# Where the first attention stage ends: its memory freed in three steps, and the layers' first projections moved between its last products

## The chip, the cores and the metric

The kernel runs on one core of a Trainium2 chip. The metric is the device time of one execution in microseconds (us); lower is better. The engines are named as in the profile: PE (matrix products; PEld is its loading of weights), DVE (vector), ACT (scalar), POOL (GpSimd) and SP, which here only issues DMAs.

## What is computed

The input x has 4 batches of 512 tokens with 128 features. It goes through a causal attention block, and then through six layers, each of a local attention (windows of 32 tokens, looking back one window) and a gated feed-forward part. The result of the six layers is added to what went into them.

```python
...
    x = x + _L0_attn_ref(_layernorm(x, axis=-1), L0_attn_Wq, L0_attn_Wk, L0_attn_Wv, L0_attn_Wr)
    x = x + _L0_ffn_ref(_layernorm(x, axis=-1), L0_ffn_Wqkv, ...)
...
        for i in range(DEPTH):
            x = attn_layer(shift_tokens(x), Wqkv[i], q_scale[i], k_scale[i], Wo[i]) + x
            x = ffn_layer(shift_tokens(x), ln_g[i], ln_b[i], W1[i], b1[i], W2[i], b2[i]) + x
```

In the first block `q`, `k` and `v` have 16 heads of 64; the softmax rows times `v` are projected out by `Wr`. In a layer `q` and `k` are divided by their norm, scaled and rotated by position before the scores. `shift_tokens` moves half of the features by one token. All is in float32, apart from masks.

## The kernel before

The program is one sequence per engine, written out by hand: inside `tc.manual_schedule()` each engine executes its instructions in the order in which the code issues them, and a tile library puts in the waits that the tiles' reads and writes ask for. When a memory pool is given back and a new one takes its place, the first users of the new tiles wait for the last users of the old ones that lie there.

Stage one (L132 to L364) works on batches b = 0 to 3 and on eight pairs of heads c = 0 to 7. A step m of its loop handles two blocks of 128 rows: scores on PE (L216), the mask as a further product (L229), row maximum on DVE (L241), exponents on ACT (L247), scaling on POOL (`normalise`, L259), and, one step later, transposes of the exponents (L270) with their copies out of PSUM by ACT (L274) and DVE (L276). Two steps later `times_v1` multiplies with V in two halves (L287) and DVE copies the result (L297). When a batch is through, `project_out1` multiplies by `Wr` (L302, 8 products that accumulate), and DVE adds the block's input (L303) to give `x1T[b]`. The layers' input is the normalised `x1T[b]`; `norm_x1` does that in three steps: mean (L93 on PE, L95 on DVE, L97 on ACT), variance (L102 on PE, then 15 small operations on DVE: L104 and `rsqrt`, L79 to L85) and scale (L110 on PE, L114 on DVE). For batches 0 to 2 the steps are spread over the next batch's loop; for batch 3 they come after the stage ("late").

[...] Stage one uses one for projections (`ps_pj`), two for transposes (`ps_pt`), four for scores (`ps_sc`), one for the product with V (`ps_o`). The layers use four for projections (`ps_proj`, two buffers of two), two for attention (`ps_att`) and two single ones (`ps_one`).

After the loop stand the rest of the products with V (L366 to L368) and the last `project_out1`. Then all of stage one's memory is given back, the layers' pools are made (L372), and POOL clears the borders of three tiles (L493, L496, L499).

The layers' work is cut into units: a unit is a layer i, a batch b and a block T of 128 tokens, 96 in all. `begin` makes the shifted input `xs` on POOL (L413 to L415) and, for batch 0, the rotation tables `lt` of the layer (a DMA of scales, L420, and one product on POOL, L422). `slot(n)` issues work of four units at once: the scores and products of unit n, the output of n-1, the transposes of q and k of n+1, the projections of n+2. Its order is the order of the code at L727 to L787. A projection (`project`, L439) is followed by Square on ACT (L450), the sum of squares (L455) and the two halves of the rotation (L460, L464) on DVE, their addition on POOL (L475), the inverse norms (DVE L479, L79, L80, then 12 small operations on POOL, L82 to L85) and the scaling by them on POOL (L483). `v_windows` copies V out on ACT (L517) and sends it by 16 DMAs on SP into overlapping windows (L525 to L529). Scores are L562 (mask) and L573, their maximum L583, the difference L585, exponents L591; the products with V are L605.

The loop starts at n = -2, so that slot -2 holds the projections of unit 0 alone, slot -1 those of unit 1 and the transposes of unit 0, and slot 0 the first scores:

```python
        for n in range(-2, len(units) + NT + 3):
            if -2 <= n < 1:
                late[n + 2]()
```

Of the kernel before, what the change touches and what calls it, by code (L numbers as in the profile page):

```python
# [8 lines left out]
F32 = mybir.dt.float32  # L9
# [3 lines left out]
ALU = mybir.AluOpType  # L13
AX = mybir.AxisListType

P = 128
HEADS = 16
HD = 64
# [13 lines left out]
def body(ctx: ExitStack, tc: tile.TileContext, a, out: bass.AP):  # L32
# [98 lines left out]

    with tc.tile_pool(name="s1", bufs=1) as s1, tc.tile_pool(  # L132
        name="ps1", bufs=1, space=bass.MemoryType.PSUM
    ) as ps1, tc.manual_schedule():
        wq = s1.tile([P, INNER], F32, tag="wq", name="wq")
        wk = s1.tile([P, INNER], F32, tag="wk", name="wk")
        wv = s1.tile([P, INNER], F32, tag="wv", name="wv")
        wr = s1.tile([P, NC, EMB], F32, tag="wr", name="wr")
        pen = s1.tile([P, S], BF16, tag="pen", name="pen")
# [13 lines left out]
        def bank1():  # L153
            return ps1.tile([P, 512], F32, tag="pj", name="ps_pj", bufs=1)

# [5 lines left out]
        def load_x(b):  # L161
            xp = pt_bank()
            for t in range(NT):
                nc.tensor.transpose(xp[:, t * P : (t + 1) * P], xr[b][:, t, :], ident)
            x0T[b] = s1.tile([P, S], F32, tag=f"x0T{b}", name=f"x0T{b}")
            nc.scalar.copy(x0T[b], xp)
# [23 lines left out]
        def make_v(b, j, t):  # L190

            if t == 0:
                vs[b, j] = s1.tile([P, NT, 512], F32, tag="v1", name="v1", bufs=3)
            p = bank1()
            mm(
                p,
                lhsT=xnT[b][:, t * P : (t + 1) * P],
                rhs=wv[:, j * 512 : (j + 1) * 512],
                start=True,
                stop=True,  # L200
            )
            nc.vector.tensor_copy(vs[b, j][:, t, :], p)

        class Rows:
# [58 lines left out]
            def transposes(self):  # L263
                b, c, t = self.b, self.c, self.t
                if t == 0:
                    pTs[b, c] = s1.tile([P, 2, NT, S], F32, tag="pT1", name="pT1", bufs=2)
                for h in range(2):
# [10 lines left out]
        def times_v1(b, c, half):  # L278

            if half == 0:  # L280
                os_[b, c] = ps1.tile([P, S], F32, tag="o1", name="ps_o1", bufs=1)
            o = os_[b, c]
# [12 lines left out]
            if half == 1:  # L295
                at = aTs[b, c] = s1.tile([P, S], F32, tag="aT1", name="aT1", bufs=NC + 2)
                nc.vector.tensor_copy(at, o)  # L297

        def project_out1(b):
            y = bank1()  # L300
            for c in range(NC):
                mm(y, lhsT=wr[:, c, :], rhs=aTs.pop((b, c)), start=(c == 0), stop=(c == NC - 1))  # L302
            nc.vector.tensor_tensor(x1T[b], y, x0T[b], ALU.add)  # L303

# [15 lines left out]
        for m in range(last + 1):  # L320
# [41 lines left out]
            if b > 0 and c == 1 and odd:  # L362
                project_out1(b - 1)
                norms1[b - 1] = norm_x1(bank1, b - 1)  # L364
            if b in range(1, B) and not odd and 4 <= c <= 6:
                norms1[b - 1][c - 4]()  # L366

        times_v1(B - 1, NC - 2, 1)  # L368
        for half in range(2):
            times_v1(B - 1, NC - 1, half)  # L370
        project_out1(B - 1)


    s2 = ctx.enter_context(tc.tile_pool(name="s2", bufs=1))
    ps = ctx.enter_context(tc.tile_pool(name="ps2", bufs=1, space=bass.MemoryType.PSUM))

# [25 lines left out]
    def one_t():  # L402
        return ps.tile([P, 512], F32, tag="one", name="ps_one", bufs=2)

# [3 lines left out]
    def flat(pt):  # L408
        return pt.rearrange("p a n -> p (a n)")

    def shift_into(dst, src):

        nc.gpsimd.memset(dst[HD:P, 0:1], 0.0)  # L413
        nc.gpsimd.tensor_copy(dst[0:HD, :], src[0:HD, :])
        nc.gpsimd.tensor_copy(dst[HD:P, 1:S], src[HD:P, 0 : S - 1])  # L415

    def layer_tables(i):

        scales = s2.tile([P, 4 * HD], F32, tag="scales", name="scales")
        nc.sync.dma_start(out=scales, in_=a["scales"][i : i + 1].to_broadcast([P, 4 * HD]))  # L420
        lt = s2.tile([P, NT, 4, HD], F32, tag="lt", name="lt", bufs=2)
        nc.gpsimd.tensor_tensor(  # L422
            lt.rearrange("p t f d -> p t (f d)"),
            tabs.rearrange("p t f d -> p t (f d)"),
            scales.unsqueeze(1).to_broadcast([P, NT, 4 * HD]),
            ALU.mult,
        )
        return lt

# [18 lines left out]
    def square(u, j):  # L448
        u.sq = s2.tile([P, INNER], F32, tag="t1", name="sq", bufs=3)
        nc.scalar.activation(u.sq, u.p[j], AF.Square)  # L450
# [6 lines left out]
    def rotate(u, j):  # L457
        t0 = u.r[j] = s2.tile([P, INNER], F32, tag="rot", name="rot", bufs=6)
        lt, pf, half = u.lt, u.p[j], HD // 2
        nc.vector.tensor_tensor(  # L460
            heads(t0), heads(pf), lt[:, u.T, 2 * j].unsqueeze(1).to_broadcast([P, HEADS, HD]), ALU.mult
        )
        t1 = u.t1 = s2.tile([P, INNER], F32, tag="t1", name="t1", bufs=3)
        nc.vector.tensor_tensor(  # L464
# [9 lines left out]
    def add_rotated(u, j):  # L474
        nc.gpsimd.tensor_tensor(u.r[j], u.r[j], u.t1, ALU.add)  # L475
# [6 lines left out]
    def over_norm(u, j):  # L482
# [5 lines left out]
        )  # L488

    kT_first = s2.tile([P, NC, W + P], F32, tag="kT_first", name="kT_first")
    nc.gpsimd.memset(kT_first[:, :, 0:W], 0.0)  # L493
    vw_first = s2.tile([P, NW, NC, HD + 1], F32, tag="vw_first", name="vw_first")
    for c in range(2):
        nc.gpsimd.memset(vw_first[c * HD : c * HD + W, 0], 0.0)  # L496
    vts = [s2.tile([P, 2, NC, HD + 1], F32, tag=f"vt{j}", name=f"vt{j}") for j in range(2)]
    for t_ in vts:
        nc.gpsimd.memset(t_[:, :, :, HD : HD + 1], 1.0)  # L499

# [5 lines left out]
    def new_vw(u):  # L506
        if u.T == 0:
            return vw_first
        return s2.tile([P, NW, NC, HD + 1], F32, tag="vw", name="vw", bufs=3)

# [29 lines left out]
    def transpose_q(u):  # L540
        u.qT = s2.tile([P, NC, P], F32, tag="qT", name="qT", bufs=1)
        for g in range(2):
            transposed(u.r[0], g, u.qT, 0)
# [168 lines left out]
    def begin(u):  # L712

        if u is None or u.T:
            return
        xs = s2.tile([P, S], F32, tag="xs", name="xs", bufs=2)
        shift_into(xs, xT[u.b])
        lt = layer_tables(u.i) if u.b == 0 else units[u.n - 1].lt
        for v in units[u.n : u.n + NT]:
            v.xs, v.lt, v.p = xs, lt, [None] * 3  # L720

    def do_project(u, j):
        u.p[j] = project(u, j)
        if u.b + 1 == B and u.T + 1 == NT and u.i + 1 < L:
            wpart[j] = load_part(u.i + 1, j)

    def slot(n, now, last):  # L727
# [8 lines left out]
        if new:  # L736
            do_project(new, 0)
            square(new, 0)
        if u:
            exponents(u)  # L740
# [35 lines left out]
        if new:  # L776
            rotate(new, 1)
            add_rotated(new, 1)
            over_norm(new, 1)
        if nxt:  # L780
            carry_k(nxt, follower(nxt))
# [7 lines left out]
    with tc.manual_schedule():  # L789
        begin(units[0])  # L790
        ffns = {}
        late = norm_x1(one_t, B - 1)
        for n in range(-2, len(units) + NT + 3):
            if -2 <= n < 1:
                late[n + 2]()
            q = n // NT - 1
# [96 lines left out]
```

## Time and profile before

| what | us |
|---|---|
| median of 3 runs | 2374.94 |
| lowest, highest run | 2371.28, 2376.27 |
| the profiled execution, its own time | 2373.12 |
| its span, first to last instruction | 2371.3 |
| end of stage one's last output product | 590.9 |
| start of the first scores of slot 0, 1, 2, 3 | 621.4, 640.6, 656.6, 673.4 |

The profile is one execution. In a timeline or chain the first number is the start in us from the span's start and the second the duration; `x8` counts instructions. PE's records count a float32 product twice. A stretch's PEclk is the share of full clock that was granted to TensorE. The slots that follow repeat in a pattern of four, some 17 to 19.5 us each, up to 2327 us.

### The profile page before, as it was taken

The numbers are of one execution on the slowest core, as the hardware profiler recorded it, in microseconds if no ns is written. First come the engines' busy times: TensorE is split into PE (matmuls) and PEld (weight loads), VectorE is DVE, ScalarE is ACT, GpSimd is POOL, SyncE is SP. The second block draws the span as 40 slices with busy tenths as digits, with TensorE's granted clock in tenths as the row PEclk, the third lists the DMA queues.
The fourth block names the chain that finished last, engine by engine and source line by source line (L and its number), as shares of the span: only waits on it lengthen the run. The fifth ranks groups of instructions, "written<-read, shape, count | busy, mean of one in ns | idle before, by whom it ended". The sixth has DMA issues, their size and how long they took to land.

```text
span 2371.3 us, 81682 instructions
## 1 busy us (share of the span) xinstructions
PE 2222.6 (94%) x35056; PEld 1448.1 (61%) x35088; DVE 1696.8 (72%) x2692; ACT 1301.6 (55%) x2166; POOL 1436.9 (61%) x1897
## 2 busy tenths in 40 slices
PE   6999999998789999999999999999999999999997
PEld 3555555554466666666666666666666666666664
DVE  3665656655778777777777778777878777777774
ACT  2554444543345566655665656566556666565662
POOL 2453434443776677666767766767766767766760
PEclk9999999999899999999999999999999999999999
DMA  3000000000222232222332223223232223322220
GB/s 110 1 1 1 1 1 1 1 1 1 62 67 57 62 91 64 64 72 59 82 73 62 65 64 87 67 62 73 68 85 63 68 59 85 77 55 69 66 59 15
DMA packets 91026, 125.82 MB, mean 53 GB/s; under 512 B 25262, under 2 KB 39468, under 8 KB 90668
## 3 DMA queue, kind: packets, MB, share of 16 engines
q1 hardware_dynamic: 90236, 119.02, 20.5%
q8 instruction: 280, 4.59, 0.9%
q10 hardware_dynamic: 432, 1.57, 0.2%
q14 instruction: 78, 0.64, 0.1%
HBM read 20.41 MB, written 1.05 MB: 9 GB/s over the span
## 4 chain that ended last, share of the span: by engine, by line
PE 77%; DVE 14%; issue 3%; ACT 3%; POOL 1%; DMA 1%; SPq 0%; ACTq 0%; POOLq 0%
PE ps_proj L439 19%; PE ps_one L535 10%; PE ps_one L630 7%; PE ps_att L605 6%; PE ps_att L573 6%; PE ps_sc L216 5%; PE ps_o L287 4%; PE ps_pt L270 3%; PE ps_proj L663 3%; PE ps_proj L664 3%; PE ps_proj L677 2%; DVE on L615 2%; DVE yt L79 2%; ACT vt L517 1%; DVE rot L460 1%
## 5 line engine op out<-in xcount | busy, mean ns | idle before, releaser
L439 PE MATMUL ps_proj<-wqkv,xs 128*128 128x512 f32 x1152 | 570.1, 618 | 31.5 <-ACT vt L517 22.9
L475 POOL TENSOR_TENSOR rot<-rot,t 128x1024 f32<-128x1024 f32 x192 | 453.3, 2361 | 199.3 <-DVE t L464 197.2
L259 POOL TENSOR_TENSOR pr<-pr,den 128x1024 f32<-128x1024 f32 x128 | 241.1, 1894 | 333.9 <-DVE den L256 331.7
L450 ACT ACTIVATE sq<-ps_proj 128x1024 f32<-128x1024 f32 x192 | 196.9, 1025 | 407.5 <-PE ps_proj L439 354.3
L483 POOL TENSOR_TENSOR rot<-rot,ss 128x1024 f32<-128x1024 f32 x192 | 365.4, 1903 | 15.1
L439 PEld LDWEIGHTS ps_proj<-wqkv,xs 128*128 128x128 f32 x1152 | 199.6, 191 | 220.1 <-issue 156.3
L455 DVE TENSOR_REDUCE ss<-sq 128x16 f32<-128x1024 f32 x192 | 233.1, 1214 | 53.8 <-ACT sq L450 53.5
L241 DVE TENSOR_REDUCE nm<-ps_sc 128x2 f32<-128x1024 f32 x128 | 156.1, 1219 | 118.8 <-PE ps_sc L229 118.8
L460 DVE TENSOR_TENSOR rot<-ps_proj,lt 128x1024 f32<-128x1024 f32 x192 | 233.6, 1217 | 0.0
L464 DVE TENSOR_TENSOR t<-ps_proj,lt 128x1024 f32<-128x1024 f32 x192 | 233.1, 1214 | 0.0
L274 ACT COPY pT<-ps_pt 128x512 f32<-128x512 f32 x128 | 75.2, 588 | 263.2 <-PE ps_pt L270 261.4
L630 PEld LDWEIGHTS ps_one<-aT,wo 128*128 128x128 f32 x1536 | 186.3, 192 | 45.3 <-issue 44.5
L82 POOL TENSOR_TENSOR yt<-y 128x32 f32<-128x32 f32 x288 | 69.3, 241 | 237.7 <-DVE y L80 222.7
L535 PE MATMUL ps_one<-ident,rot 128*128 128x128 f32 x1536 | 211.3, 281 | 0.8 <-ACT qT L538 0.7
L583 DVE TENSOR_REDUCE mx<-ps_att 128x16 f32<-128x1024 f32 x96 | 117.6, 1225 | 119.8 <-PE ps_att L573 119.8
L630 PE MATMUL ps_one<-aT,wo 128*128 128x128 f32 x1536 | 187.3, 275 | 0.4 <-ACT aT L538 0.4
L247 ACT ACTIVATE pr<-ps_sc,nm 128x512 f32<-128x512 f32 x256 | 175.0, 695 | 16.5 <-DVE nm L241 16.5
L535 PEld LDWEIGHTS ps_one<-ident,rot 128*128 128x128 f32 x1536 | 165.7, 142 | 20.5 <-issue 2.9
L614 DVE RECIPROCAL rden<-ps_att 128x8 f32<-128x8 f32 x192 | 39.6, 206 | 193.5 <-PE ps_att L605 192.0
L605 PEld LDWEIGHTS ps_att<-vw,pT 64*32 64x32 f32 x9216 | 105.1, 105 | 106.4 <-issue 72.8
L605 PE MATMUL ps_att<-vw,pT 64*32 64x65 f32 x9216 | 129.0, 225 | 35.5 <-DVE on L615 28.9
L270 PEld LDWEIGHTS ps_pt<-ident,pr 128*128 128x128 f32 x1024 | 119.2, 141 | 55.3 <-issue 44.9
(127 smaller groups left out, 4042.1 us busy)
## 6 DMA issues: line engine op xcount, KB each, us to landing
vw<-vt SPq DMA_DIRECT2D x1152, 65.0 KB
vw_first<-vt SPq DMA_DIRECT2D x336, 65.0 KB
wqkv<-in_wqkv_dram SPq DMA_DIRECT2D x18, 512.0 KB
wo<-in_wo_dram SPq DMA_DIRECT2D x6, 512.0 KB
w<-in_w_dram SPq DMA_DIRECT2D x6, 341.0 KB
xr<-in_x_dram SPq DMA_DIRECT2D x4, 256.0 KB
out_dram<-tmp_t SPq DMA_DIRECT2D x4, 256.0 KB
w<-in_w_dram SPq DMA_DIRECT2D x12, 64.0 KB
```

Source lines behind the costliest of these rows:

```text
L259: nc.gpsimd.tensor_tensor(self.pr, self.pr, self.den.unsqueeze(2).to_broadcast([P, 2, S]), ALU.mult)
L270: nc.tensor.transpose(pt[:, k * P : (k + 1) * P], self.pr[:, h, k * P : (k + 1) * P], ident)
L439: mm(p[:, c, :], lhsT=u.xs[:, u.T * P : (u.T + 1) * P], rhs=wpart[j][:, c * 512 : (c + 1) * 512], start=True, stop=True,)
L450: nc.scalar.activation(u.sq, u.p[j], AF.Square)
L455: nc.vector.tensor_reduce(u.ss[:, j * HEADS : (j + 1) * HEADS], heads(u.sq), AX.X, ALU.add)
L460: nc.vector.tensor_tensor(heads(t0), heads(pf), lt[:, u.T, 2 * j].unsqueeze(1).to_broadcast([P, HEADS, HD]), ALU.mult)
L464: nc.vector.tensor_tensor(t1.rearrange("p (h t d) -> p h t d", t=2, d=half), pf.rearrange("p (h t d) -> p h t d", t=2, d=half)[:, :, ::-1, :],
L475: nc.gpsimd.tensor_tensor(u.r[j], u.r[j], u.t1, ALU.add)
L483: nc.gpsimd.tensor_tensor(heads(u.r[j]), heads(u.r[j]), u.ss[:, j * HEADS : (j + 1) * HEADS].unsqueeze(2).to_broadcast([P, HEADS, HD]), AL ...
L535: nc.tensor.transpose(tp[:, c * P : (c + 1) * P], src[:, (4 * g + c) * P : (4 * g + c + 1) * P], ident)
L605: mm(o[j * W : (j + 1) * W, h, c * (HD + 1) : (c + 1) * (HD + 1)], lhsT=u.pT[h * HD : (h + 1) * HD, 4 * g + c, j * W : (j + 1) * W], rhs=u ...
L630: mm(y[:, 0:P], lhsT=wo_w[0][:, c, :], rhs=u.aT[:, c, :], start=(c == 0), stop=(c == NC - 1))
```

## The change

Stage one's memory pools are split in three, `s1`, `s1b` and `s1c`, and given back at three places. The first place is the end of the loop; after it `s2a` and `ps2` (tiles of projection, Square and rotation; PSUM of projections and attention) come to stand where `s1` was. The second is after the last product with V (`second_step`), which gives room to `s2b` and the single banks. The third is after the last residual (`third_step`). The start tile `xs` and the tables of unit 0 move into a pool of their own and are made in the loop, at b = 3, c = 2.

A `first_slot` takes the place of slot -2. It issues unit 0's projections with the last three halves of the products with V between them, and the projection of V after that of K. The border clears are issued after the inverse norms. In slot -1 the last output product stands after unit 1's first projection and goes to the attention bank; its residual stands at the end of the slot's DVE work. The late steps of the norm move from slots -2, -1, 0 to slots 0, 1, 2.

```diff
+    pre = ctx.enter_context(tc.tile_pool(name="pre", bufs=1))
+    steps = [ExitStack() for _ in range(3)]
+    s1c = steps[2].enter_context(tc.tile_pool(name="s1c", bufs=1, side="right"))
+    s1b = steps[1].enter_context(tc.tile_pool(name="s1b", bufs=1, side="right"))
+    ps1b = steps[1].enter_context(tc.tile_pool(name="ps1b", bufs=1, space=PSUM, side="right"))
+    s1 = steps[0].enter_context(tc.tile_pool(name="s1", bufs=1))
+    ps1 = steps[0].enter_context(tc.tile_pool(name="ps1", bufs=1, space=PSUM))
...
+    def shifted(b):
+        xs = pre.tile([P, S], F32, tag="xs", name="xs", bufs=2)
+        shift_into(xs, xT[b])
+        return xs
...
-        def project_out1(b):
-            y = bank1()
+        def project_out1(b, y):
             for c in range(NC):
                 mm(y, lhsT=wr[:, c, :], rhs=aTs.pop((b, c)), start=(c == 0), stop=(c == NC - 1))
+
+        def residual1(b, y):
             nc.vector.tensor_tensor(x1T[b], y, x0T[b], ALU.add)
...
-
-        times_v1(B - 1, NC - 2, 1)
-        for half in range(2):
-            times_v1(B - 1, NC - 1, half)
-        project_out1(B - 1)
...
+            if b == B - 1 and c == 2 and not odd:
+                start = shifted(0), layer_tables(0)
+        steps[0].close()
...
+    def second_step():
...
+        steps[1].close()
+        s2b = ctx.enter_context(tc.tile_pool(name="s2b", bufs=1))
+        ps_one = ctx.enter_context(tc.tile_pool(name="ps2b", bufs=1, space=PSUM))
...
+        for t_ in vts:
+            nc.gpsimd.memset(t_[:, :, :, HD : HD + 1], 1.0)
+        vw_first = s2b.tile([P, NW, NC, HD + 1], F32, tag="vw_first", name="vw_first")
+        for c in range(2):
+            nc.gpsimd.memset(vw_first[c * HD : c * HD + W, 0], 0.0)
+        kT_first = s2b.tile([P, NC, W + P], F32, tag="kT_first", name="kT_first")
+        nc.gpsimd.memset(kT_first[:, :, 0:W], 0.0)
+
+    def third_step():
...
+        steps[2].close()
+        s2 = ctx.enter_context(tc.tile_pool(name="s2", bufs=1))
...
+    def first_slot():
+
+        new = units[0]
+        do_project(new, 0)
+        square(new, 0)
+        times_v1(B - 1, NC - 2, 1)
+        rotate(new, 0)
+        sum_squares(new, 0)
+        add_rotated(new, 0)
+        do_project(new, 1)
+        times_v1(B - 1, NC - 1, 0)
+        square(new, 1)
+        rotate(new, 1)
+        sum_squares(new, 1)
+        add_rotated(new, 1)
+        inverse_norms(new)
+        times_v1(B - 1, NC - 1, 1)
+        second_step()
+        over_norm(new, 0)
+        over_norm(new, 1)
+        do_project(new, 2)
+        v_windows(new, units[1])
 
     def slot(n, now, last):
...
         if new:
             do_project(new, 0)
             square(new, 0)
+        if n == -1:
+            y = att_t()[:, 0, :]
+            project_out1(B - 1, y)
...
             rotate(new, 1)
             add_rotated(new, 1)
             over_norm(new, 1)
+        if n == -1:
+            residual1(B - 1, y)
+            third_step()
...
-        for n in range(-2, len(units) + NT + 3):
-            if -2 <= n < 1:
-                late[n + 2]()
+        first_slot()
+        for n in range(-1, len(units) + NT + 3):
+            if 0 <= n < 3:
+                late[n]()
```

## The prediction

> **What bounds the kernel now.** I read the page first: PE is the busiest engine by far, in both halves.
>
> ```profile
> PE 2222.6 (94%) x35056; PEld 1448.1 (61%) x35088; DVE 1696.8 (72%) x2692; ACT 1301.6 (55%) x2166; POOL 1436.9 (61%) x1897
> ```
>
> So only PE's gaps can be won, and the change touches one place, the seam between the stages (577 to 657 us). The stretches of the seam (columns: us; busy time and instructions of PE, PEld, DVE, ACT, POOL; granted clock; DMA share; GB/s) show where the gaps lie.
>
> ```profile
> 577.30:590.90 13.60, 12.69 (x41) 4.71 (x40) 2.08 (x3) 0.29 (x1) 0.00 (x0) 1.00 0.00 0
> 590.90:621.40 30.50, 21.56 (x60) 9.53 (x61) 19.90 (x29) 8.92 (x13) 16.49 (x25) 0.78 0.27 64
> 621.40:640.60 19.20, 14.98 (x309) 9.19 (x308) 15.65 (x22) 7.62 (x12) 15.91 (x23) 0.91 0.25 58
> 640.60:656.60 16.00, 15.05 (x330) 10.42 (x328) 11.85 (x17) 8.33 (x14) 11.70 (x18) 1.00 0.26 62
> ```
>
> In the first row PE works alone; in the second it idles 9 us and has 0.78 of its clock. The last row is an undisturbed slot, 16.0 us. The chain of waits tells why (start, us, what):
>
> ```profile
> 583.81 7.08 PE ps_pj L302 x16
> ...
> 594.23 0.62 POOL xs L415
> 594.85 0.04 issue
> 594.90 6.65 PE ps_proj L439 x8
> ...
> 607.03 0.19 DVE ss L479
> ...
> 607.46 0.18 DVE y L80
> 607.65 1.13 DVE rot L460
> 608.77 1.13 DVE t L464
> 609.90 0.08 DVE rs L104
> ...
> 611.78 1.77 DVE yt L84
> 613.57 2.28 DVE y L85
> ...
> 616.07 1.76 DVE yt L83
> ...
> 627.38 1.15 DVE mx L583
> 628.55 1.23 DVE pr L585
> 629.80 1.06 ACT pr L591
> 630.91 1.18 PE ps_one L535 x7
> ```
>
> Two things are to be seen. The projections start 4 us after the output product (L302), behind memsets and shift on POOL. And from 605.78 DVE has no gap until the maximum (L583): the late norm's variance (L104 to its last L85) stands in it for 8.3 us, though it is 15 tiny operations; three of them take 1.8 to 2.3 us.
>
> [...] the L84, L85 and L83 above end at 613.54, 615.84 and 617.82, when POOL's L483 (to 613.51), L475 (to 615.82) and L483 (to 617.81) end; the same lines take 0.16 to 0.25 us otherwise. [...] the trace has half clock at 594.0 to 600.8, 611.1 to 617.9 and 631.6 to 635.0, multiples of 3.41 us, each after a gap. [...]
>
> **The change, part by part.** All times are on the clock of before, so that they can be set beside it. Durations: a projection takes PE 1.72 us (1.98 to its last result), a half of the product with V 1.72, the output product 6.87; two rotations 2.3, a sum of squares 1.13, Square 1.02, the pair of V copies 1.07, POOL's addition 2.35, its scaling 1.9, its inverse roots 3.8 (L82 at 607.73 to 611.53).
>
> *Start tile and tables (4 POOL instructions, 1 DMA).* In stage one, at batch 3, c = 2, 0.09+0.60+0.61+2.34 plus gaps = 3.8 us. POOL idles 4.21 us there (491.30 to 495.51), so 0. If the cover is short, the scaling of the scores comes up to 1 us late; its transposes have slack of more than 1 us. I keep 0 to 1. The scales' DMA now waits for no memory and runs at the start.
>
> *Front.* PE's transposes end at 577.4. The first projection takes over the transposes' PSUM, so it waits for the last copy out (DVE, 578.13): PE loses 0.8. Then, in PE's order: projection 578.2 to 579.9; product 6 second half to 581.65; projection 1 to 583.4; product 7 (its bank free after the copy on DVE, 582.6) to 586.8; projection 2 to 588.5; unit 1's first projection (buffer free when the second rotation ends, 588.5) to 590.3; the output product to 597.2; unit 1's V and K projections to 600.6. PE has no gap and no reason for half clock: the two slow projections (6.65 for 8 records, at 2 x 1.72 = 3.44 otherwise) lose their 3.2 us.
>
> *DVE and POOL below it.* DVE: copy 6 to 582.6, rotation 0 to 584.9, squares to 586.0, rotation 1 to 588.5 (its second half waits for the addition on POOL, 587.2), squares to 589.6. The next operation, L479, is small and meets POOL's second addition (to 590.9): 1.2 us lost, as L479 at 622.77 took 1.33. Inverse roots on POOL 591.4 to 595.2, the five memsets 1.6 (591.80 to 593.39 before) to 596.9, two scalings to 600.7. These are needed by the transposes at 600.6: about on time. The first V DMA waits for a memset, 595.3; 16 at 0.63 us end at 605.4, needed at about 617. The Square and V copies on ACT are done by 591.6. For unit 1: sum of squares waits for Square of the K projection (601.9), 603.2; three small operations 603.85; rotation 606.1; residual 606.7. Only then the mean's product on PE: idle from 603.7 to 606.75. Scores of slot 0 start at 607.6 against 621.4 (band product, L562). Here I let PE fall to half clock once and charge 0.9. Maximum to first transposes cost 3.6 as before (627.29 to 630.91): they start at 614.6 against 630.91. **Gain 16.3.**
>
> *Rest of slot 0.* Before, 631.6 to 635.0 was at half clock, and the rest took 9.7 (630.91 to 640.65); slot 1 took 8.9 (647.71 to 656.59). After, 8.9: slot 0's body ends at 623.5 against 640.65. **Gain 17.1.**
>
> *The late norm.* Its three steps move from slots -2, -1, 0 to 0, 1, 2. The mean is counted above. The variance: 8 records on PE (1.1 us) ahead of the scores, 15 small operations on DVE ahead of slot 1's maximum. POOL's queue at that point is the same as before: inverse roots, scaling, addition, scaling, each blocking one of them. So I take the old pattern: from L80 (607.46) to the variance's end (618.22) 10.8, then 3.6 to the transposes: 14.4. Without it slot 1 has L80 at 639.76 and its transposes at 647.71: 7.95. **Loss 6.4**; PE stands still for some 5 us of it, which brings a window of half clock, priced from slot 0 of before (9.7 against 8.9): **loss 0.9**. Bounds: 1.1 (no blocking: 15 x 0.2 = 3 us, hidden behind 5.3 us of projections and output product) and 10 (the full pattern, with two half-clock windows of 1.7 us). The scale step in slot 2: 4 transposes on PE, **loss 0.65**; its DVE operation (0.68) lies before the maximum with slack.
>
> *All later.* In the built programs the instructions stand in the same order on every engine from then on. 0.
>
> Sum: 17.1 - 6.4 - 0.9 - 0.65 = 9.1; less 0.1 for stage one, 9.0. The profiled execution took 2373.1 (span 2371.3 and 1.8 around it): 2364.1. The median of the runs is 1.8 higher, so I forecast 2366.0.
>
> **The rivals.**
> 1. *The variance is hidden.* For it: in a later slot (802.7 to 806.9) the same 15 operations took 4.2, since POOL ran out of work. Against: there they stand after the maximum; at the slot's start POOL has three long instructions due. Gain 17.1 - 1.1 - 0.65, about 15.4: 2359.5.
> 2. *Half clock eats more of it.* Both waits of PE (before slot 0 and in slot 1) bring two windows instead of one: up to 1.7 us each, on top, and the front's waits another 1.5. Gain about 4: 2371. For it: 594.0 to 600.8 held two windows although PE was busy from 594.9. Against: most of a slot's small products lose less than the projections.
> 3. *Slower: PE stays at half clock over slots 0 to 2.* At half rate a slot's three projections and its output product lose up to 4 x 1.7 = 6.9 us, so PE is late for its own next wait. It decides beyond 1.3 slots (9.0/6.9), about 23 us at half clock; two slots in full give 13.8 - 9.0 = 4.8 slower, 2380. Against: before, each busy stretch released it after one or two windows.
> 4. That the change doesn't do what it says: the built order excludes it; the V products do follow the projection.
>
> **How the numbers follow.** Forecast (2362 to 2370) 0.60; rival 1 0.16; rival 2 0.18; rival 3 0.06. From the forecast's own range I move 0.04 to within 0.2% (4.7 us, about what a measurement of this kernel can tell from no change); rival 2 splits 0.05 faster, 0.12 same, 0.01 slower. Faster 0.56+0.16+0.05 = 0.77, same 0.16, slower 0.07. The range reaches from rival 1 to just beyond rival 2: 2358.5 to 2372.5; it leaves out rival 3 and the edges of the others.
>
> **What would show it.** Right: no gap on PE over 1 us between 578 and 602; slot 0's first transposes some 16 us earlier; in slot 1 three or more small DVE operations of 1.7 to 2.3 us between rotation and maximum, and PE idle for 5 us there; from slot 3 on a constant offset of about 9. Wrong: a stall of the projections on a PSUM release I took as met, the first scores later than 612, a slot 1 of under 18 us (rival 1), or offsets that go on changing after slot 3.

## The result, and the profile after

The changed kernel takes 2367.88 us (median of 22 runs, 2361.24 to 2373.56), the kernel before 2374.85 (22 runs, 2370.02 to 2381.89). The ratio is 0.9969, with a 95% interval of 0.996 to 0.9979: 7.0 us or 0.31% less. The forecast was 9.0 us. The profiled execution of the changed kernel took 2366.26, its span 2364.4. Lines of the code have moved: the projection is now L456, Square L467, sum of squares L472, rotation L477 and L481, inverse norm L496, POOL's addition L492 and scaling L500, transposes L564, scores L591 and L602, maximum L612, exponents L620, products with V of the layers L634, residual of stage one L338.

The page of the changed kernel has the same work on every engine in a shorter span:

```profile
PE 2223.6 (94%) x35088; PEld 1446.2 (61%) x35088; DVE 1693.3 (72%) x2692; ACT 1301.5 (55%) x2166; POOL 1435.1 (61%) x1897
```

The stretches of the seam, with columns as in the prediction (us; busy time and count of PE, PEld, DVE, ACT, POOL; clock; DMA share; GB/s), now cut at the end of stage one's transposes, the start of the output product, and the first scores of slots 0, 1, 2 and 3:

```profile
577.65:591.30 13.65, 12.82 (x42) 4.55 (x42) 9.24 (x9) 3.31 (x5) 4.43 (x2) 1.00 0.00 0
591.30:608.90 17.60, 13.53 (x45) 6.43 (x44) 9.30 (x14) 5.16 (x8) 13.69 (x34) 0.99 0.28 69
608.90:625.00 16.10, 15.18 (x317) 10.11 (x316) 11.92 (x16) 8.79 (x14) 11.36 (x14) 0.90 0.40 95
625.00:648.66 23.66, 18.27 (x329) 12.09 (x328) 19.20 (x32) 8.46 (x13) 11.44 (x17) 0.86 0.24 58
648.66:664.20 15.54, 14.80 (x325) 10.38 (x324) 11.39 (x17) 7.54 (x12) 11.02 (x15) 1.00 0.21 50
```

DVE, ACT and POOL now work beside PE's last products (first row), and full clock holds until the first scores. The price stands in the fourth row: slot 1 took 23.66 us, PE idle for over 5 of them. The chain of waits (start, us, what) runs through PE almost without a break to 601, then through unit 1's Square, squares and inverse norm, and in slot 1 through the late norm's variance:

```profile
578.48 1.96 PE ps_proj L456 x4
...
591.43 6.87 PE ps_att L335 x16
...
601.82 1.03 ACT sq L467
...
625.33 0.08 DVE rs L104
...
627.19 1.77 DVE yt L84
628.98 2.28 DVE y L85
...
631.48 1.76 DVE yt L83
...
633.78 1.14 DVE mx L612
...
637.31 1.97 PE ps_one L564 x8
639.28 3.41 PE ps_proj L456 x4
```

The three blocked operations, each ending 0.01 to 0.02 us after a long one of POOL's, are of L84, L85 and L83, the lines that were blocked before; the maximum now stands right behind them. The projection after the transposes took 3.41 us for its 4 records where the one at 578.48 took 1.96: half clock (a clock of 0.50 from 635.9 to 642.7). From 607 to 615 the chain is drawn over SP's DMAs of V; they don't bind there, for with the residual early (below) they are issued at the same time after stage one, and slot 0 comes 3 us sooner.

The ledger of the two profiled executions, each on its own clock:

| start of | before | after | gained | forecast |
|---|---|---|---|---|
| scores, slot 0 | 621.4 | 608.9 | 12.5 | 13.8 |
| transposes of exponents, slot 0 | 630.9 | 615.7 | 15.2 | 16.3 |
| scores, slot 1 | 640.6 | 625.0 | 15.6 | 17.1 |
| transposes of exponents, slot 1 | 647.7 | 637.3 | 10.4 | 10.7 |
| scores, slot 2 | 656.6 | 648.7 | 7.9 | 9.15 |
| scores, slot 3 | 673.4 | 664.2 | 9.2 | 9.1 |
| scores, slot 4 | 690.9 | 682.0 | 8.9 | 9.1 |
| end of the span | 2371.3 | 2364.4 | 6.9 | 9.0 |

### The profile page after: what moved, and what is told of

The parts are those of the page before. It is cut to its first block, busy times and chain, and to the rows that moved or that the text cites. A ratio compares the mean times of both kernels' runs of the same rounds, so it can differ in the third digit from the quotient of the medians.

```text
span 2364.4 us, 81715 instructions
## 1 busy us (share of the span) xinstructions
PE 2223.6 (94%) x35088; PEld 1446.2 (61%) x35088; DVE 1693.3 (72%) x2692; ACT 1301.5 (55%) x2166; POOL 1435.1 (61%) x1897
## 3 DMA queue, kind: packets, MB, share of 16 engines
q8 instruction: 280, 4.59, 0.9%
## 4 chain that ended last, share of the span: by engine, by line
PE 78%; DVE 14%; ACT 3%; issue 3%; DMA 1%; POOL 1%; SPq 0%; ACTq 0%; POOLq 0%
PE ps_proj L456 19%; PE ps_one L564 10%; PE ps_one L659 7%; PE ps_att L634 6%; PE ps_att L602 6%; PE ps_sc L250 5%; PE ps_o L321 4%; PE ps_pt L304 3%; PE ps_proj L692 3%; PE ps_proj L693 3%; PE ps_proj L706 2%; DVE on L644 2%; PE ps_sc L263 2%; DVE yt L79 2%; PE ps_att L591 1%
## 5 line engine op out<-in xcount | busy, mean ns | idle before, releaser
L456 PE MATMUL ps_proj<-wqkv,xs 128*128 128x512 f32 x1152 | 564.6, 613 | 22.5 <-ACT vt L546 20.3
L492 POOL TENSOR_TENSOR rot<-rot,t 128x1024 f32<-128x1024 f32 x192 | 453.0, 2359 | 205.4 <-DVE t L481 203.5
L467 ACT ACTIVATE sq<-ps_proj 128x1024 f32<-128x1024 f32 x192 | 196.9, 1026 | 405.0 <-PE ps_proj L456 356.4
L500 POOL TENSOR_TENSOR rot<-rot,ss 128x1024 f32<-128x1024 f32 x192 | 365.3, 1903 | 14.9
L456 PEld LDWEIGHTS ps_proj<-wqkv,xs 128*128 128x128 f32 x1152 | 198.5, 190 | 207.2 <-issue 153.1
L472 DVE TENSOR_REDUCE ss<-sq 128x16 f32<-128x1024 f32 x192 | 233.0, 1214 | 52.2 <-ACT sq L467 51.7
L477 DVE TENSOR_TENSOR rot<-ps_proj,lt 128x1024 f32<-128x1024 f32 x192 | 233.5, 1216 | 0.0
L481 DVE TENSOR_TENSOR t<-ps_proj,lt 128x1024 f32<-128x1024 f32 x192 | 232.9, 1213 | 0.4 <-POOL rot L492 0.4
L82 POOL TENSOR_TENSOR yt<-y 128x32 f32<-128x32 f32 x288 | 69.0, 239 | 243.8 <-DVE y L80 228.8
L659 PEld LDWEIGHTS ps_one<-aT,wo 128*128 128x128 f32 x1536 | 186.3, 192 | 45.3 <-issue 44.5
L564 PE MATMUL ps_one<-ident,rot 128*128 128x128 f32 x1536 | 209.6, 279 | 1.0 <-POOL rot L492 0.9
L612 DVE TENSOR_REDUCE mx<-ps_att 128x16 f32<-128x1024 f32 x96 | 117.5, 1224 | 121.7 <-PE ps_att L602 119.9
L281 ACT ACTIVATE pr<-ps_sc,nm 128x512 f32<-128x512 f32 x256 | 175.0, 694 | 16.9 <-DVE nm L275 16.9
L564 PEld LDWEIGHTS ps_one<-ident,rot 128*128 128x128 f32 x1536 | 164.5, 141 | 19.9 <-issue 2.2
L634 PEld LDWEIGHTS ps_att<-vw,pT 64*32 64x32 f32 x9216 | 104.8, 105 | 108.2 <-issue 71.2
L634 PE MATMUL ps_att<-vw,pT 64*32 64x65 f32 x9216 | 128.5, 224 | 36.7 <-DVE on L644 29.4
```

The source lines that it names most:

```text
L456: mm(p[:, c, :], lhsT=u.xs[:, u.T * P : (u.T + 1) * P], rhs=wpart[j][:, c * 512 : (c + 1) * 512], start=True, stop=True,)
L472: nc.vector.tensor_reduce(u.ss[:, j * HEADS : (j + 1) * HEADS], heads(u.sq), AX.X, ALU.add)
L477: nc.vector.tensor_tensor(heads(t0), heads(pf), lt[:, u.T, 2 * j].unsqueeze(1).to_broadcast([P, HEADS, HD]), ALU.mult)
L481: nc.vector.tensor_tensor(t1.rearrange("p (h t d) -> p h t d", t=2, d=half), pf.rearrange("p (h t d) -> p h t d", t=2, d=half)[:, :, ::-1, :],
L500: nc.gpsimd.tensor_tensor(heads(u.r[j]), heads(u.r[j]), u.ss[:, j * HEADS : (j + 1) * HEADS].unsqueeze(2).to_broadcast([P, HEADS, HD]), AL ...
L564: nc.tensor.transpose(tp[:, c * P : (c + 1) * P], src[:, (4 * g + c) * P : (4 * g + c + 1) * P], ident)
```

## The experiments

The theory: the gain of the front is some 15 us, and the late norm's variance, a chain of tiny DVE operations that wait for POOL's long ones ahead of slot 1's maximum, gives back 6.4 of it, with half clock on top. The rivals: slot 1 is long by half clock or by PE's extra products, or the front's gain comes from the moved output product or the early start tile alone. The medians are of 4 to 22 executions. Single executions of one kernel differ by some 10 us, and in each profile windows of half clock fall in other places, so each experiment is read in two ways: its ratio to the kernel before on the same chip, and its seam, counted from the end of stage one's last transposes in its profile. The table has the starts of the scores of slots 0, 1, 2 and 4 (S0 to S4) and of the transposes of slots 0 and 1 (T0, T1), in us, and the median and ratio [95% interval].

| kernel | S0 | T0 | S1 | T1 | S2 | S4 | median, ratio |
|---|---|---|---|---|---|---|---|
| before | 44.0 | 53.5 | 63.2 | 70.3 | 79.2 | 113.5 | |
| before, again | 44.0 | 53.6 | 63.4 | 70.6 | 79.6 | 114.0 | 2370.06, 0.9999 [0.9988, 1.001] |
| after | 31.2 | 38.1 | 47.4 | 59.7 | 71.0 | 104.3 | 2367.88, 0.9969 [0.996, 0.9979] |
| after, again | 32.1 | 39.0 | 48.4 | 60.7 | 72.0 | 104.7 | 2364.96, 0.9973 [0.9966, 0.9981] |
| variance behind the maximum | 31.1 | 38.1 | 46.2 | 54.3 | 65.3 | 98.1 | 2358.58, 0.9953 [0.9938, 0.9968] |
| variance's roots on POOL | 31.3 | 38.1 | 47.4 | 54.5 | 64.2 | 100.5 | 2358.95, 0.9946 [0.9932, 0.996] |
| before, variance in slot 1 | 40.7 | 47.6 | 55.7 | 63.8 | 77.2 | 109.6 | 2369.91, 0.9995 [0.9985, 1.0004] |
| variance twice | 32.1 | 39.0 | 49.5 | 63.7 | 75.3 | 107.5 | 2367.23, 0.9988 [0.998, 0.9997] |
| output product first | 33.5 | 39.7 | 49.2 | 61.6 | 72.1 | 104.9 | 2365.75, 0.9982 [0.9975, 0.9989] |
| start tile at the end | 33.9 | 40.2 | 49.4 | 61.7 | 72.6 | 105.4 | 2366.09, 0.9979 [0.9968, 0.999] |
| residual early | 28.2 | 34.1 | 43.5 | 56.2 | 66.4 | 99.4 | 2360.09, 0.9961 [0.9945, 0.9976] |
| residual early, variance behind | 28.2 | 34.1 | 42.2 | 50.3 | 62.9 | 95.2 | 2355.99, 0.9941 [0.9926, 0.9956] |
| PE kept busy | 32.1 | 38.7 | 48.1 | 60.7 | 69.4 | 102.4 | 2361.57, 0.9964 [0.995, 0.9978] |
| all roots on POOL | 28.2 | 34.5 | 42.6 | 50.7 | 60.2 | 93.4 | 2326.08, 0.9815 [0.9797, 0.9834] |

The kernel before measured 2371.39 beside the first four experiments, 2370.18 beside the next four, and 2371.15 beside the two repeats and the last two (35 runs each).

**The two repeats.** Both kernels once more, for the spread of the seam.

> The kernel before, unchanged, for a second profile on the chip that also runs the three others of this set. All theories: within 0.1% of itself. It shows how far the seam's own length changes from one execution to the next: I expect the scores of slot 4 some 110 to 114 us after stage one's last transposes, as the windows of half clock fall (113.5 in the first profile).

> The changed kernel, unchanged, a second profile beside the kernel before on one chip. Theory (the gain lies in the seam alone): scores of slot 4 about 104 us after stage one's last transposes as in the first profile, 7 to 9 us less than the kernel before on this chip, and the time 6 to 9 us less. Rival (part of the gain in the seam is given back at the end of the kernel, where the first profile lost 1.9 us): the time gains 2 us or more less than the seam.

Up to slot 4 the change gained 9.2 us in the first pair of profiles and 9.2 in the second; the starts repeat within 0.5 us (before) and 1.0 us (after). A difference in the seam of 2 us or more can be read. The whole time gained 6.4 us by the ratio, nearly 3 less than the seam, as the rival says, but not at the end of the kernel, where the second pair differs by 0.3 us only. Every kernel with an edit but the last (all roots on POOL) also gained less in the whole time than in its seam, by 0.4 to 5 us, so the seam's gain is not to be taken for that of the whole.

**Variance behind the maximum.**

```diff
-            if 0 <= n < 3:
+            if n in (0, 2):
                 late[n]()
...
             (now.mean, now.var, now.scale)[T - 1]()
+        if n == 1:
+            late[1]()
```

> The changed kernel with one thing moved: the late norm's variance in slot 1 is issued where a feed-forward norm has it, behind the maximum and the residual, instead of ahead of the scores. Theory (the variance's small operations, blocked by POOL, hold back slot 1's maximum): the loss of 6.4 us of waiting and of the half clock behind it goes, and some 2 us come back because the same operations now delay the rotation of unit 3; slot 1 falls from 23.7 us to about 18, the scores of slot 3 start near 658.5 instead of 664.2, the time is about 6 us under the changed kernel's 2367.9, near 2362. Rival (slot 1 is long because the front has left other work over, DMAs or POOL): slot 1 stays above 22 us and the time within 2 us of the changed kernel.

T1 comes 5.4 us earlier than in after, S4 6.2 earlier. The ratio moves the same way, but its interval overlaps those of after. DVE's timeline of slot 1 in this kernel (start, us, engine, line, operation, names, shapes):

```profile
626.03 1.22 DVE L612 TENSOR_REDUCE mx<-ps_att 128x16 f32<-128x1024 f32 x1 [0.48 <-PE ps_att L602]
...
630.19 0.28 DVE L667 TENSOR_TENSOR xT<-ps_one,xT 128x128 f32<-128x128 f32 x1
630.51 0.16 DVE L104 TENSOR_SCALAR rs<-ps_one 128x4 f32<-128x4 f32 x1
630.71 0.76 DVE L79 TENSOR_SCALAR yt<-rs 128x4 int32<-128x4 int32 x1
...
631.71 1.75 DVE L82 TENSOR_TENSOR yt<-y 128x4 f32<-128x4 f32 x1
```

The maximum waits for PE's scores alone. The chain is the same but meets only the end of POOL's addition and one scaling: L79 ends at 631.47 and L82 at 633.46, POOL's two at 631.44 and 633.43. What the chain cost in slot 1 was set by its place. Slot 1 took 19.1 us, not 18: PE now waited 1.63 us for a division that stands behind the chain.

**Variance's roots on POOL.** The chain keeps its place, but its last 12 operations go to POOL.

```diff
-            rsqrt(rs, NT, nc.vector)
+            rsqrt(rs, NT, eng)
...
-        late = norm_x1(one_t, B - 1)
+        late = norm_x1(one_t, B - 1, nc.gpsimd)
```

> The changed kernel, the variance at its place, but its 12 root operations issued on POOL; DVE keeps 3. POOL runs them in its own queue behind slot 0's last copy. Theory (blocking of small DVE operations behind POOL's long ones, not the amount of work): DVE has nothing left to be blocked, slot 1's transposes start about 7.5 to 8 us after its scores instead of 12.3, PE keeps full clock, slot 1 takes about 16.5 us, the time is some 7 to 8 us under the changed kernel's, near 2360. Rival (the steps are simply that much work, and POOL is no freer): POOL's addition for unit 3 comes 3.8 us later and passes the delay on; slot 1 over 19 us and less than 4 us gained.

Slot 1 fell to 16.9 us, as blocking predicts. In DVE's timeline the two root operations left do not wait at all:

```profile
625.72 0.24 DVE L79 TENSOR_SCALAR yt<-rs 128x4 int32<-128x4 int32 x1
625.99 0.17 DVE L80 TENSOR_SCALAR y<-yt 128x4 int32<-128x4 int32 x1
627.24 1.22 DVE L612 TENSOR_REDUCE mx<-ps_att 128x16 f32<-128x1024 f32 x1 [1.07 <-PE ps_att L602]
```

At S4 only 3.8 us of the 6.8 at S2 were left: slot 2 took 19.1, with a break of 1.71 us in the middle of PE's scores, for which the profile shows no wait, and a window of half clock behind it (for such breaks see the end).

**Before, with the variance in slot 1.** One part of the change alone, on the kernel before, in the better place.

```diff
-            if -2 <= n < 1:
-                late[n + 2]()
+            if n in (-2, 2):
+                late[max(n, 0)]()
...
             (now.mean, now.var, now.scale)[T - 1]()
+        if n == 1:
+            late[1]()
```

> The kernel before with one part of the change's idea alone: the late norm's variance taken out of slot -1 and issued in slot 1 behind the maximum, the scale step in slot 2; memory, projections and output product as before. Theory (in the kernel before the variance was 8.3 us of the chain on DVE, and it is not hidden there): DVE reaches slot 0's maximum about 6 to 8 us earlier, less 2 us for its new place: 4 to 6 us under the kernel before, near 2369.5, so that much of what the whole change gave could be had without touching the memory. Rival (PE's late start bounds that stretch and the variance was in its shadow): within 2 us of the kernel before, 2375.

Slot 0's transposes came 5.9 us earlier, S4 3.9 earlier, but the median fell by only 1.5 us, which can't be told from nothing (0.9995 [0.9985, 1.0004]). On the time the rival was nearer. Slot 1 grew to 21.5 us, because here the chain stands in front of the division of the last output, for which PE's next products wait:

```profile
650.12 1.19 PE L605 MATMUL ps_att<-vw,pT 64*32 64x65 f32 x64 [3.45 <-DVE on L615]
```

So the tiny chain costs wherever PE needs DVE behind it. At S0 this step alone gained 3.3 us of the whole change's 12.7, at T0 5.9 of 15.4. The rest of the front's gain is put down to the overlap with stage one's products; no run took that overlap alone away.

**Variance twice.** The step is issued a second time ahead of slot 1's maximum and computes the same values again.

```diff
                 late[n]()
+            if n == 1:
+                late[1]()
```

> The changed kernel with the variance step of slot 1 issued twice in a row; the second repeats the first. Theory (the cost comes from three long POOL instructions, each of which blocks one small operation, and these have run out when the first variance ends): the second costs its bare work, 15 operations at 0.2 us and 8 records on PE, about 3 to 4.5 us on top: slot 1 about 27.5 us, the time near 2372. Rival (the small operations are slow by themselves, 8.4 us for 15): 8 us or more on top, near 2376.

T1 came 3.0 to 4.0 us later than in the two profiles of after, S4 2.8 to 3.2. The second chain ran from 636.18 to 639.05, 15 operations in 2.87 us with none over 0.17: POOL's three long operations were done at 635.70. That is the prediction's "15 x 0.2 = 3 us", and it shows that of the first chain's 8.5 us some 5.6 are waiting. Slot 1 took 25.8 us, less than the 27.5 expected.

**Output product first.** In `first_slot` it is put back right behind the last product with V.

```diff
         times_v1(B - 1, NC - 1, 1)
+        y = att_t()[:, 0, :]
+        project_out1(B - 1, y)
         second_step()
...
-        if n == -1:
-            y = att_t()[:, 0, :]
-            project_out1(B - 1, y)
```

> The changed kernel with the last output product back in its old place on PE, straight behind the last product with V and so ahead of unit 0's V projection and unit 1's projections; memory, start tile and the residual's place stay. Theory (the order does not matter by itself; what counts is that PE has no gap): PE's work up to 601.6 is the same in sum and stays without a gap; unit 1's first projection ends 7 us later, DVE has 7 us of slack there, so 0 to 1 us is lost: near 2368.5. Rival (the gain comes from the projections standing ahead of the output product, as the change's words say): 5 to 7 us lost, near 2374.

S0 is 1.4 to 2.3 us later than in after, S4 0.2 to 0.6. A wait of 1.16 us for a V copy comes back between the projections, and most of the delay is made up later. By the ratio 2 to 3 us of the gain are gone, but the intervals overlap. In the seam, where the output product stands hardly matters, as long as other products fill PE.

**Start tile at the end.** Start tile and tables are issued behind the loop.

```diff
-            if b == B - 1 and c == 2 and not odd:
-                start = shifted(0), layer_tables(0)
+        start = shifted(0), layer_tables(0)
         steps[0].close()
```

> The changed kernel with the start tile and the tables of unit 0 issued on POOL at the end of stage one's loop instead of 11 steps earlier; they keep their own memory. Theory (POOL is idle from 576.5 on and the first projection waits for PSUM until 578.4 anyway): start tile done at 577.9, tables at 580.3, the rotation needs them at 583: 0, within 1 us of the changed kernel. Rival (POOL's chain ahead of the first projection is what the change removed, 4 us before): 1.5 to 4 us lost.

The first projection waited 0.98 us instead of 0.83; it fell into a window of half clock (3.58 us for 1.96), which makes up most of S0's 1.8 to 2.6 us. PE was busy for 49% of the 3.41 us before that; in after the same gaps fell into two such stretches, 64% (from 574.46) and 82% busy (from 577.87), both at full clock. S4 is 0.6 to 1.1 later, less than the seam can show, and the ratio's interval overlaps those of after. The early place is not what the gain rests on.

**Residual early.** `residual1` is issued behind slot -1's first rotation, so that slot 0's mean need not wait for unit 1's rotation.

```diff
         if new:
             rotate(new, 0)
+        if n == -1:
+            residual1(B - 1, y)
...
         if n == -1:
-            residual1(B - 1, y)
             third_step()
```

> The changed kernel with the last residual moved up on DVE in slot -1, behind unit 1's first rotation instead of behind its second. Theory (PE's wait of 3.2 us ahead of slot 0, and the half clock after it, come from the residual's place in DVE's queue): the residual ends near 599, slot 0's scores start near 605.5 instead of 608.9, its transposes near 611.5 instead of 615.7; about 4 us under the changed kernel, near 2364. Rival (DVE's queue up to the maximum is the bound, and PE's wait is only its shadow): the maximum moves by less than 1 us and so does the time.

The wait ahead of the mean's product, 3.22 us in after, is 0.24 here. PE's timeline in after, then in this kernel:

```profile
607.75 1.22 PE L93 MATMUL ps_one<-x1T,avg 128*128 128x512 f32 x2 [3.22 <-DVE x1T L338]
```

```profile
605.78 1.13 PE L93 MATMUL ps_one<-x1T,avg 128*128 128x512 f32 x2 [0.24 <-ACT kT_first L567]
```

S0 is 3.1 to 3.9 us earlier and S4 4.9 to 5.3, for slot 0 then ran at full clock too (5.9 us from S0 to T0, where after took 6.9). In the ratio the gain is 2 to 3 us, with intervals that overlap.

**Residual early, variance behind the maximum.** Both edits.

> Both moves on the changed kernel: the residual early in slot -1, the variance behind slot 1's maximum. Theory (they are two separate waits): the gains add, 4 and 6 us, the time near 2358. Rival (they are the same DVE backlog, met in two places): no more than the larger of the two, near 2362.

S4 is 9.1 to 9.5 us earlier than in after; the two edits gave 4.9 and 6.2 apart. They add up but for 2 us, and here the ratio's interval lies wholly under those of after.

**PE kept busy.** After, with 34 transposes of the identity, whose result nobody reads, where PE waits in slot 1.

```diff
+        if n == 1:
+            idle = one_t()
+            for _ in range(34):
+                nc.tensor.transpose(idle[:, 0:P], ident, ident)
```

> The changed kernel with 34 transposes of the identity on PE in slot 1, behind the V projection, whose result nobody reads; they fill about 4 of the 4.9 us for which PE waits there. Theory (that wait brings half clock, which makes the rest of slot 1 some 2 us longer): the first transposes of slot 1 stay where they are (59.7 us after stage one's end), slot 2's scores come after 9 us instead of 11.3; 1.5 to 2.5 us less. Rival (the rest of slot 1 is long for another reason): no change, or 1 us more if the filling is late.

PE's timeline in slot 1 of after, then of this kernel:

```profile
639.07 3.62 PE L456 MATMUL ps_proj<-wqkv,xs 128*128 128x512 f32 x4
```

```profile
633.72 3.88 PE L817 MATMUL ps_one<-ident 128*128 128x128 f32 x34
639.22 1.06 PE L564 MATMUL ps_one<-ident,pr 128*128 128x128 f32 x8 [1.63 <-DVE xT L667]
640.12 1.88 PE L456 MATMUL ps_proj<-wqkv,xs 128*128 128x512 f32 x4
```

T1 is unchanged (60.7 in both on this chip), so the products cost nothing; from T1 to S2 it takes 8.7 us instead of 11.3. Half clock in slot 1 cost 2.6 us. That the whole time gains is not settled: the two ratios' intervals overlap.

**All roots on POOL.** The last combination, with the inverse root of every norm of the program moved, on top of the two edits.

```diff
-            rsqrt(rs, NT, nc.vector)
+            rsqrt(rs, NT, nc.gpsimd)
```

> The kernel with the early residual and the late variance behind the maximum, and now the 12 root operations of every layer norm (24 feed-forward norms, 8 in stage one) issued on POOL instead of DVE. Theory (the small operations on DVE, 4.2 us each time and more where POOL blocks them, lengthen every fourth slot to 19.4 us against 17.2 to 17.8): those slots lose 1 to 1.6 us, 24 times: 24 to 38 us less, the time near 2325. Rival (PE bounds those slots, or POOL's queue takes the delay over): less than 8 us.

This is the best version: 2326.08 us (4 executions), 45.1 less than before, though POOL has more work. The page of this kernel, busy time and then the chain's shares:

```profile
PE 2223.1 (96%) x35088; PEld 1447.0 (62%) x35088; DVE 1625.7 (70%) x2308; ACT 1301.0 (56%) x2166; POOL 1513.5 (65%) x2281
...
PE 87%; ACT 4%; DVE 4%; issue 3%; DMA 1%; POOL 0%; ACTq 0%; SPq 0%; POOLq 0%
```

The same line of the changed kernel:

```profile
PE 78%; DVE 14%; ACT 3%; issue 3%; DMA 1%; POOL 1%; SPq 0%; ACTq 0%; POOLq 0%
```

PE's work is the same; DVE's share of the chain fell from 14% to 4%. Against the second profile of after, on the same chip, stage one ends 10.4 us earlier (567.9 against 578.3), the seam up to S4 is 11.3 shorter, and the slots from 4 to 95 are 12.5 shorter. Against the kernel with the two edits alone (on another chip) the roots' move gives 29.7 us: 10.1 in stage one, 1.8 in the seam, 14.8 in the slots from 4 to 95 and 3.0 at the end.

The sum is within the 24 to 38 us expected, but by luck: all of it was forecast for every fourth slot. Those that hold a norm's roots (10 to 38) took 18.4 to 19.4 us instead of 19.4 to 19.6, and over all 23 the gain was 0.64 each, not 1 to 1.6. Stage one, for which nothing was forecast, gains in six steps of 1.7 to 1.9 us, one at a norm each. In five of them PE's wait of 1.8 us for a V copy on DVE goes. PE's timeline at one, with the two edits and then in this kernel:

```profile
214.65 1.12 PE L220 MATMUL ps_pj<-xnT,wk 128*128 128x512 f32 x2 [1.82 <-DVE v L236]
```

```profile
211.65 1.12 PE L220 MATMUL ps_pj<-xnT,wk 128*128 128x512 f32 x2
```

There it is the chain's own work, not blocking, that goes from DVE's queue: the 12 operations took DVE 2.3 us (209.92 to 212.18), and the one before them, which POOL held up (1.79 us), is the same in both kernels.

## Why the prediction was right, and where its sizes were off

*Right: the front.* PE had no gap over 1 us between 578 and 602, the only one being the 0.83 us for the transposes' PSUM that the prediction charged. Both slow projections regained full clock. L496, held up by POOL's second addition, took 1.31 us at 590.31 (1.2 lost in the forecast); the two end at 591.62 and 591.59. PE waited 3.22 us for the last residual (603.7 to 606.75 in the forecast). The start tile cost nothing that shows: the changed kernel was 0.27 us late at 487 already, before POOL came to it, and 0.25 at stage one's end (0.93 and 0.93 in the second pair).

*Right: the late norm.* From L80 (622.89) to the transposes (637.31) it took 14.42 us, 14.4 forecast. Moving the chain, shortening it and doubling it all show the same cause. In the profile of after L84, L85 and L83, with 4 elements a row, end at 628.95, 631.25 and 633.23, and POOL's L500, L492 and L500 at 628.93, 631.23 and 633.22. Between L85 and L83 DVE got in one operation, L82 (0.16 us at 631.28). Not every operation is held up: with the variance behind the maximum L472, a reduction, took its usual 1.22 us and L667, with one input in PSUM, 0.28 (at 629.06 and 630.19), beside an L492 that ran from 629.09 to 631.44. What decides which are held up was not shown; that slot 1 would repeat what the profile before showed was the author's estimate. POOL's timeline in after:

```profile
627.02 1.91 POOL L500 TENSOR_TENSOR rot<-rot,ss 128x1024 f32<-128x1024 f32 x1
628.89 2.34 POOL L492 TENSOR_TENSOR rot<-rot,t 128x1024 f32<-128x1024 f32 x1
631.31 1.91 POOL L500 TENSOR_TENSOR rot<-rot,ss 128x1024 f32<-128x1024 f32 x1
```

*Mis-sized: the front's durations.* "Scores of slot 0 start at 607.6" came at 608.9. The projections ended at 601.7 instead of 600.6: I chained them by 1.72 us, and between products of different kinds PE took some 1.9 (578.48 to 580.37 to 582.24). This term is 1.1 us.

*Mis-sized: half clock.* "I let PE fall to half clock once and charge 0.9" for slot 0 was right: 608.6 to 612.0, one window, and 6.8 us from scores to transposes against 5.9 in the kernel with the residual early, at full clock there. Slot 1's "loss 0.9" was too small. There were two windows, 635.9 to 642.7; from T1 to S2 it took 11.35 us, 0.65 of it the scale step, against 8.9: 1.8, and 2.6 by the run with PE kept busy. I took the price from slot 0 of before, where a window covered one projection; here the transposes were slow as well (1.97 against 1.04). And slot 1 of before, from which I counted, had two waits of PE of its own in that stretch (0.29 us at 649.04, 0.32 at 653.80), which hid 0.6 us of the price. This is rival 2 in small.

*Failed: "All later. 0".* At S2 the gain was 7.9, not 9.15. The two terms above ask for 2.0 us less; 0.8 of it had come back in slot 0, which took 7.2 us from the transposes to L80, where the forecast's sum has 8.0. At S3 the gain was 9.2. The 1.3 us between came back because slot 2 of before had a break in its scores (1.10 us at 658.88, with no wait in the profile) and slot 2 of after had none; the second pair shows the same (1.10 at 659.3, and none). So the match at S3 is partly luck: a term that was put at nothing made up for two that were too small.

Then the last slots and the tail took 1.9 us more (46.4 against 44.5 from the last scores to the end), with half clock at 2346 to 2353 in the profile of after. In the second pair the tails differ by 0.3 and the spans by 8.1. Over all 14 profiles this tail took 44.4 to 44.9 us in the 8 where half clock came there in single windows of 3.4 us, and 46.4 to 48.1 in the 6 where it came in double ones. All 6 are of kernels with the changed seam; none of the three profiles with the old front has a double window. Whether that is chance was not shown. The 6.9 of the first pair, the 8.1 of the second and the interval of the ratio (5.0 to 9.5 us) fit a gain of the seam of 9 less what is lost elsewhere.

*The rivals.* Hiding the variance (rival 1) was out, slot 1 taking 23.7 us and not under 18. Rival 3 needed 23 us at half clock; the seam had 10.2 (3.4 and 6.8).

## What to carry to other kernels

Before you move a chain of tiny vector operations, look at what GpSimd runs at its new place and at what stands behind it in VectorE's queue: in slot 1 the chain's cost was mostly the rest of GpSimd's long instructions (some 5.6 of 8.5 us), in stage one it was its own length, with PE waiting behind it. Overlapping the two stages paid where it filled PE; the order within the filled stretch mattered little. And slot 1's PE wait of 4.9 us cost more than itself: the half clock after it took 2.6 us.

## What was not expected of the hardware

- Moving 12 operations of each norm from DVE to POOL, where one takes 0.20 instead of 0.16 us, gained far more than the change that was studied: 0.9815 against 0.9941 for the same kernel without it. A third of that came in stage one, where nothing was forecast.
- Half clock came in windows of 3.41 us. In the profiles of before and after they start whole multiples of 3.41 us apart (594.0, 611.1 and 631.6 in before; 608.6, 635.9 and 2346.0 in after). What followed a window went with how busy PE was in it: in the 14 profiles (from 100 us to 10 us before the end) full clock followed all 73 windows of half clock in which PE was busy for 86% or more, and none of the 22 with 80% or less (in before and after alone, all 10 with 98% or more and none of the 4 with 74% or less). In slot 1 of after half clock lasted from 635.9 to 642.7, though PE worked from 637.31 on: the first window was 59% busy. Half clock came without an idle window, too: it followed 73 windows, in which PE was busy for 44% at the median, and up to 71% in all but one (in before and after alone, 10 windows of 0 to 67%).
- PE stopped for 1 us and more, mostly in runs of small products, with nothing in the profile that it waits for (1.67 us before 676.88 in before, 1.72 before 667.94 in after). This is less random than it looks: one such stop stands in slot 3 of all 14 profiles, in slot 5 of 13. From 600 us on the profiles have 103 such breaks of over 0.5 us, and every one ends 1.2 to 1.7 us after the end of a transfer on the queue that the profile's page lists as `q8 instruction: 280, 4.59, 0.9%` (in before and after alone, 19 breaks, 1.2 to 1.5 us), though these come only every 7 us in the mean. Whether PE waits for these transfers was not shown: no run moved one.
